# A four-layer gated network on one core: context work of three sequences kept for the sorted experts of layer 0, their rare branch issued first, and a denser schedule of table writes in layer 1

## The chip, the core and the metric

The kernel runs on one core of a Trainium2 chip, in one launch. The time is what the device takes for one execution, in microseconds (us). Before the change it is 2764.47 us in the median of three runs (2760.23 to 2768.61).

The engines in the profile are PE (matrix products, with its weight loads listed as PEld), DVE (vector), ACT (activations), POOL (GpSimd) and SP, which only issues DMAs. Each works through its own list of instructions in order. Lists are laid down when the kernel is built: the scheduler gives every instruction a priority by its place in the program, takes the first one that is ready by its own reckoning, and writes the semaphore waits that correctness needs.

## What is computed

Eight sequences of 256 tokens, 512 channels wide, pass through four layers. Each layer adds a gated attention over a context of the same shape, then a gated feed-forward part. Only layer 0 and the first half of layer 1 bear on the change:

```python
x = x + tanh(g_xattn[0]) * L0_xattn(layernorm(x), ctx)      # 16 heads, 8-bit rounding of the queries and the output
x = x + tanh(g_ffn[0])   * L0_ffn(layernorm(x))             # 8 experts of rank 64, each token takes the best one
x = x + tanh(g_xattn[1]) * L1_xattn(layernorm(x), ctx)      # linear attention
x = x + tanh(g_ffn[1])   * L1_ffn(layernorm(x))             # 64 experts, each token takes 8
...
# L1_xattn
k_prime = relu(key_heads @ Wkf.T)                            # 64 features a head
kv      = einsum('bhnf,bhne->bhfe', k_prime, v)
out     = einsum('bhmf,bhfe->bhme', q_prime, kv) / (q_prime . k_sum + 1e-8)
```

The keys, features and sums (`k_prime`, `kv`) of layer 1's linear attention depend on the context alone, not on the tokens.

## The kernel before

The tokens are held in 16 tiles `xt` of 128 tokens. Three stages follow one another: `front` (layer 0), `middle` (layer 1) and `back` (layers 2 and 3). Much of the kernel is written as Python generators: work that is off the main path is cut into pieces by `yield`, and the main path calls `next` on it at chosen points. A piece that is called early comes early in the program, and so has priority over what is called later.

**Attention of layer 0.** `attend0` (L773 on) takes one sequence: four groups of four heads, each with score products (L796), a masked maximum on DVE (L816), exponentials on ACT (L821), turns on PE (L828) and products with the values (L837). After each head it calls `step`, 16 times in a sequence. `step` moves the projection of the sequence before (`proj`) by one piece and, at the sequence's `rate`, the generator `others(b)` by one piece or two. `others` mixes what the next sequence needs (queries, keys, values), the routing `route0` of the one before, and the context work `linear(b - 1)` for b of 2 to 7.

**Context work.** `linear(b)` (L374 on) makes layer 1's keys (two pieces, products L219, ACT L329), values (two pieces, DVE L384), features (two pieces, products L398, DVE L406) and sums (two pieces, products L421, DVE L428) of sequence b, and stores the sums in DRAM as `kvd[b]` (L430), from where layer 1 loads them (L1094). Eight pieces and a store in all. The last sequence's is the generator `last_side`: one piece goes into the projection of the last sequence, two into its routing, the rest into `sorted0`.

**Sorted experts.** `route0` writes, for two tiles of tokens at a time, number and weight of each token into rows of a table in DRAM, by indirect DMAs on POOL (L513). `sorted0` counts the tokens of each expert (L624), reads the slices of the table that are used (L647), turns them on PE (`who_ps`, L678) into `who` and `share`, and goes over tiles of 128 tokens in pairs. Each tile is gathered by an indirect DMA on POOL (L688) and turned (L197); `up` (L715) and `down` (L727) are the two products; the result is scaled (L734, L736) and written to `res0` in DRAM by an indirect DMA on POOL (L737). Eight pairs are fixed, two more always run with expert weights gathered on POOL (L702), and up to ten further tiles stand in a branch, `tc.If(tiles > MORE0_ANY)`, at the end. Its condition is a count that each engine loads into a register of its own. Where the branch is not taken, each engine adds to the semaphores what the skipped part would have added; POOL first waits for its own open DMAs.

**From layer 0 to layer 1.** `results0`, called from `attend1` of the first block, reads `res0` back (L1077, SP) and adds it to the tokens: the first four tiles on DVE, the other twelve on POOL (both L1085). Small tiles of layer 1 lie in memory that tiles of layer 0 had, so they wait until those are free.

**Layer 1.** `attend1` takes four blocks of 512 tokens. It calls `step(n)` after each part, 20 writes' worth in a block; a call moves `work()`, the routing `route1` of earlier half blocks (13 pieces for each of seven), by one piece, and issues up to n writes to layer 1's table (L1188, indirect DMAs on POOL, 128 in all, 16 for each half block). `hurry`, in the second half of the last block, makes that two rounds. Each write waits for the newest product (`latest`). Each routing begins with a norm that needs a power on POOL (L172). After the blocks, the rest of `work()` runs, then the shared expert of three blocks in 13 pieces with up to three writes behind each; the routing of the last half block goes beside it and then writes all that is left. The table is read on POOL (L1422), turned on PE (L1438), and layer 1's experts begin.

Of the kernel before, what the change touches and what calls it, by code (L numbers as in the profile page):

```python
# [11 lines left out]
F32 = mybir.dt.float32  # L12
# [3 lines left out]
ALU = mybir.AluOpType  # L16
# [4 lines left out]
P = 128  # L21
# [26 lines left out]
def flamingo_kernel(ctx: ExitStack, tc: tile.TileContext, a):  # L48
# [214 lines left out]

    def front():
# [51 lines left out]

        def keys(b, bank, w=None, bias=None, out=None, name="k0"):

            out = K if out is None else out
            w, bias = (wkT, bk) if w is None else (w, bias)  # L320
            out[b] = qkv.tile([P, KC, S], F32, tag="qkv", name=f"{name}_{b}")
            for h in range(2):
                ps = bank(f"{name}ps{b}_{h}").rearrange("p (n t) -> p n t", n=2)
                for n in range(2):
                    j = 2 * h + n
                    matmul_k(ps[:, n], [w[:, k, ts(j, P)] for k in range(KC)], [ctxs[b][:, k, :] for k in range(KC)])
                for n in range(2):
# [50 lines left out]
        def linear(b, bank):  # L378

            yield from keys(b, bank, wk1, bk1, K1, "k1")  # L380
            for lt in range(2):
                ps = bank(f"v1_{b}_{lt}")
                matmul_k(ps, [ctxs[b][:, k, ts(lt, P)] for k in range(KC)], [wv1[:, k, :] for k in range(KC)])
# [156 lines left out]
        def others(b):  # L540
# [17 lines left out]
            def context():  # L558
                if b + 1 < B:
                    yield from keys(b + 1, actile)  # L560
                    yield from values(b + 1, actile)
                if b > 1:
                    yield from linear(b - 1, actile)
# [24 lines left out]
        rate = (0.9, 0.9, *(5 * (1.7,)), 1.3)  # L588
        last_side = linear(B - 1, mmtile)
# [18 lines left out]
        for n, _ in enumerate(proj[0]):  # L608
            if n == 1:
                next(last_side)  # L610
# [3 lines left out]
        for n, _ in enumerate(rest):  # L614
            if n in (1, 2):
                next(last_side)
        sorted0(AB, xnd, table, halves, writes, run, onesb, side, part, pair_no, more_no, is_more, tile_no, last_side)

    def sorted0(AB, xnd, table, halves, writes, run, onesb, lp, part, static_row, more_no, is_more, tile_no, filler):
# [54 lines left out]
        next(filler)  # L674
        next(filler)
# [46 lines left out]

        def down(nm, hT, Bs, ns, free=True):
            ps = [mmtile(f"y0_{nm}_{n}") for n in range(2)]
            last = None
            for n in range(2):
                one = nc.tensor.matmul(ps[n], hT[half[n], :], Bs[n], start=True, stop=True)  # L727
                if last is not None:
                    behind(one, last, "two experts side by side")
                last = one  # L730
            for n, i in enumerate(ns):
# [17 lines left out]

        rest = None  # L750
        static = [(c, t) for t in range(2) for c in range(4)]
        for c, t in static:
# [6 lines left out]
            next(filler, None)  # L759

        def more_pair(m, rest, free):
            ns = [16 + m, 16 + m + 1]
            xgTs = [gathered(i) for i in ns]
            ws = [weights(m + n) for n in range(2)]
            hT = up(f"m{m}", xgTs, [w[0] for w in ws])
            if rest is not None:
                down(*rest)
            return f"m{m}", hT, [w[1] for w in ws], ns, free
# [3 lines left out]
        down(*rest)  # L772
        for _ in filler:  # L773
            pass
        with tc.If(tiles > MORE0_ANY):
            rest = None
            for m in range(MORE0_ANY, MORE0, 2):
                rest = more_pair(m, rest, False)
            down(*rest)
# [168 lines left out]
    def middle():  # L948
        with ExitStack() as st:
# [123 lines left out]
            def results0(tiles, eng):  # L1073

                for t in tiles:
                    more = t2.tile([P, C], F32, tag="t2", name=f"res0_{t}")
                    load = nc.sync.dma_start(more, res0[ts(t, P), :])  # L1077
                    for one in done0:
                        tc.add_manual_dep(
                            load.ins,  # L1080
                            one.ins.name,
                            mybir.DependencyInfo(mybir.DependencyClass.Sync, mybir.DependencyReason.DATA),
                            reason="every token's result is there",
                        )
                    eng.tensor_tensor(out=xt[t], in0=xt[t], in1=more, op=ALU.add)  # L1085
# [1293 lines left out]
```

## Time and profile before

| | |
|---|---|
| median of three runs | 2764.47 us |
| the profiled execution | 2741.27 us |
| its span, first to last instruction | 2739.6 us |
| mean granted PE clock | 0.961 |
| PE busy | 2504.7 us, 91% |
| PE weight loads busy | 1371.3 us, 50% |
| DVE busy | 1302.5 us, 48% |
| POOL busy | 979.8 us, 36% |
| ACT busy | 678.1 us, 25% |

The profiled execution is 23 us faster than the median of the runs beside it; parts of it are to be compared with each other, not with the median.

Stages in this execution: layer 0's attention to 567 us, its routing and experts to 661, layer 1's attention from 685 to 905, layer 1's shared expert and last routing to 971, its experts from 1010 on. DMA engines are busy for 0.9 and more of the time in the experts of layer 1 and for under 0.25 in both attentions. Layer 1's 128 table writes take 126.9 us on POOL, 991 ns each in the mean, with 0.3 us between two that follow one another; the 16 result loads of layer 0 land 4.6 us after issue in the median.

A timeline line gives start, duration, engine, line of the program, instruction, output and inputs, shape and count, and in brackets the idle time before it with what ended it. PE's ends are modelled, and neighbouring products overlap in it.

### The profile page before, as it was taken

The page shows a single profiled execution, that of the slowest core. Times are in us where ns is not written, and L with a number is a line of the kernel's source. Part 1 is how long each engine was busy: PE and PEld are TensorE (multiplying, and loading weights), DVE is VectorE, ACT ScalarE, POOL GpSimd, SP SyncE. Part 2 cuts the span into 40 slices and gives each one's busy share as a digit, 9 for nine tenths or more (in the row PEclk, how much of TensorE's full clock was granted, in tenths as well). Part 3 has the DMA queues.
Part 4 walks back from the last instruction along what each step waited for, and adds up shares of the span by engine and source line. Part 5 has one row for each costly group of instructions (what it writes and reads, how often), then busy time and mean ns, then how long its engine had stood idle before and what let it go on. Part 6 is the DMA issues. An engine that isn't in the chain of part 4 may idle for free. (4 is left out here: it accounts for less than half of the span.)

```text
span 2739.6 us, 29988 instructions
## 1 busy us (share of the span) xinstructions
PE 2504.7 (91%) x10207; PEld 1371.3 (50%) x10215; DVE 1302.5 (48%) x3652; ACT 678.1 (25%) x1567; POOL 979.8 (36%) x915
## 2 busy tenths in 40 slices
PE   8888888966999839999999899899999899999997
PEld 6555555543555415555555344444444444455554
DVE  6666666543476812222222471567677765111111
ACT  2443434311112203232323220222212221111110
POOL 1121111136344665555555210131434252433332
PEclk9999999978799869999999999999999999999999
DMA  5000001045121228999998542112022211788984
GB/s 214 13 12 24 24 24 47 16 115 180 36 78 51 78 97 219 232 243 237 245 230 227 139 189 73 58 70 100 31 92 79 99 34 46 240 283 270 300 278 112
DMA packets 107942, 351.79 MB, mean 128 GB/s; under 512 B 23759, under 2 KB 26321, under 8 KB 100869
## 3 DMA queue, kind: packets, MB, share of 16 engines
q0 software_dynamic: 49920, 166.53, 23.8%
q1 hardware_dynamic: 54596, 178.99, 18.5%
q10 hardware_dynamic: 3264, 4.24, 0.5%
q8 instruction: 86, 1.41, 0.2%
q14 instruction: 76, 0.61, 0.1%
HBM read 289.47 MB, written 76.66 MB: 134 GB/s over the span
## 5 line engine op out<-in xcount | busy, mean ns | idle before, releaser
L219 PE MATMUL gu<-w,eb 128*128 128x352 f32 x896 | 286.4, 463 | 0.0
L1541 POOL DMA_INDIRECT acc<-eb,who x112 | 176.9, 1580 | 189.9 <-ACT eb L110 165.7
L219 PE MATMUL h2p<-xnT_f,p 128*128 128x512 f32 x512 | 226.2, 596 | 6.7 <-issue 6.0
L219 PE MATMUL o2f<-p,h 128*128 128x512 f32 x512 | 226.0, 595 | 3.5 <-ACT h L1699 3.4
L219 PEld LDWEIGHTS gu<-w,eb 128*128 128x128 f32 x896 | 162.5, 192 | 73.6 <-issue 2.3
L821 ACT ACTIVATE pr<-pr,n 128x256 f32<-128x256 f32 x256 | 128.4, 503 | 152.4 <-DVE n L816 133.4
L219 PEld LDWEIGHTS h2p<-xnT_f,p 128*128 128x128 f32 x512 | 96.7, 191 | 123.9 <-issue 121.3
L219 PEld LDWEIGHTS o2f<-p,h 128*128 128x128 f32 x512 | 95.7, 190 | 122.8 <-issue 114.7
L1188 POOL DMA_INDIRECT table<-pay,rowi x128 | 126.9, 991 | 83.7 <-issue 29.7
L1461 POOL DMA_INDIRECT xg<-xnd,who x112 | 116.5, 1040 | 49.6 <-PE ehp L1488 19.2
L197 PEld LDWEIGHTS tr_xg<-ident,xg 128*128 128x128 f32 x672 | 77.0, 142 | 111.9 <-issue 55.2
L197 PE MATMUL tr_xg<-ident,xg 128*128 128x128 f32 x672 | 116.5, 285 | 8.2 <-DMA xg<-xnd,who 8.2
L1532 PE MATMUL ed<-w,eb 128*128 128x512 f32 x224 | 116.1, 600 | 0.9 <-DVE eb L1489 0.9
L2043 PE MATMUL g_r<-w,xgT 128*128 128x352 f32 x288 | 111.2, 468 | 0.8 <-DVE xgT L108 0.8
L230 DVE SCALAR_TENSOR_TENSOR x<-o2f,tg,x 128x512 f32<-128x512 f32 x64 | 46.9, 741 | 136.8 <-PE o2f L219 135.3
L2043 PE MATMUL u_r<-w,xgT 128*128 128x352 f32 x288 | 108.7, 459 | 0.0
L816 DVE CUSTOM_DVE_ANT_0 pr<-s,mask 128x256 f32<-128x256 f32 x256 | 99.1, 417 | 13.5 <-PE s L796 5.9
L2066 PE MATMUL d_r<-w,hT_r 128*128 128x512 f32 (+1 forms) x216 | 104.2, 592 | 0.0
L1478 DVE SCALAR_TENSOR_TENSOR eb<-eb,share,gu 128x176 f32<-128x176 f32 x112 | 44.0, 393 | 121.1 <-ACT eb L1477 121.1
L108 DVE COPY eb<-ed 128x512 f32<-128x512 f32 x56 | 38.7, 692 | 129.9 <-PE ed L1532 129.9
L1699 ACT ACTIVATE h<-h2p,b 128x512 f32<-128x512 f32 x64 | 43.4, 687 | 215.9 <-PE h2p L219 215.7
L828 PE MATMUL pt<-ident,pr 128*128 128x128 f32 x512 | 88.9, 290 | 6.9 <-ACT pr L821 3.6
(702 smaller groups left out, 4722.3 us busy)
## 6 DMA issues: line engine op xcount, KB each, us to landing
w<-in_w SPq DMA_DIRECT2D x64, 960.0 KB, 6.9
p<-in_p SPq DMA_DIRECT2D x64, 512.0 KB, 5.4
xnd<-xn_f SPq DMA_DIRECT2D x32, 256.0 KB, 3.0
acc<-xnd SPq DMA_DIRECT2D x32, 256.0 KB, 4.6
more<-acc SPq DMA_DIRECT2D x32, 256.0 KB, 5.3
wd<-in_wd SPq DMA_DIRECT2D x64, 96.0 KB
ctx<-in_ctxT SPq DMA_DIRECT2D x8, 512.0 KB, 3.5
x<-in_x SPq DMA_DIRECT2D x16, 256.0 KB, 6.0
```

The source lines that it names most:

```text
L197: one = nc.tensor.transpose(ps[:, k, :], src[:, ts(k, P)], ident)
L219: one = nc.tensor.matmul(ps, lhsT[k], rhs[k], start=(k == 0), stop=(k == n - 1))
L230: return nc.vector.scalar_tensor_tensor(xt[i], ps, scale, xt[i], ALU.mult, ALU.add)
L816: one = nc.vector.tensor_tensor_reduce(pr[:, nt, :], ps[r][:, nt, :], mask[:, nt, :], -1.0, -LOW, ALU.add, ALU.min, n16[:, nt, h : h + 1],)
L821: nc.scalar.activation(pr[:, nt, :], pr[:, nt, :], AF.Exp, bias=n16[:, nt, h : h + 1], scale=-1.0, accum_out=s16[:, nt, h : h + 1],)
L828: nc.tensor.transpose(pt_ps[:, lt, nt, :], pr[:, nt, ts(lt, P)], ident)
L1188: one = nc.gpsimd.indirect_dma_start(out=table[:, :], out_offset=bass.IndirectOffsetOnAxis(ap=rows, axis=0), in_=choice, in_offset=None, b ...
L1461: nc.gpsimd.indirect_dma_start(out=xg, out_offset=None, in_=xnd[:, :], in_offset=bass.IndirectOffsetOnAxis(ap=who[:, c : c + 1], axis=0), ...
L1532: one = nc.tensor.matmul(ps[n], t.hT[rows, k, :], wd, start=(k == 0), stop=(k == 1))
L1541: nc.gpsimd.indirect_dma_start(out=acc[n][:, :], out_offset=bass.IndirectOffsetOnAxis(ap=who[:, t.c : t.c + 1], axis=0), in_=t.x, in_offse ...
L2043: nc.tensor.matmul(ps[:, 0:I3], xTt[:, k, :], wgu[k][:, g, :], start=(k == 0), stop=(k == KC - 1))
L2066: one = nc.tensor.matmul(ps, hT[:cn, n, :], wd[n][:cn], start=(n == 0), stop=(n == 2))
```

## The change

It has five parts.

1. `others` no longer runs `linear` for b of 6 and 7, so the context work of sequences 5 and 6 is not in layer 0's attention. `last_side` runs over sequences 5, 6 and 7. The rates of the last two sequences go from 1.7 and 1.3 to 1.3 and 0.5.
2. Its pieces are spread anew: five in the last projection (one before), three in the last routing (two before), which together are sequence 5; seven behind the table's read (two before); none between the fixed pairs of experts (one for each before); the other nine behind the last pair. The key and value products of these last ones are ordered on PE behind the last `down` product (`hold`, `held`).
3. The branch is issued ahead of the fixed pairs, not behind everything.
4. The first four tiles' `results0` is called in `sorted0`, behind the last pair and ahead of those nine pieces. The other twelve stay where they were.
5. In layer 1's attention a call of `step` moves the routing by 1.4 pieces (2 with `hurry`, as before) and issues up to 2n writes.

```diff
@@ front
+        hold = []
+        def held(one):
+            for other in hold:
+                behind(one, other, "the experts first")
...
-                    matmul_k(ps[:, n], [w[:, k, ts(j, P)] for k in range(KC)], [ctxs[b][:, k, :] for k in range(KC)])
+                    one = matmul_k(ps[:, n], [w[:, k, ts(j, P)] for k in range(KC)], [ctxs[b][:, k, :] for k in range(KC)])
+                    held(one)
...
-                if b > 1:
+                if 1 < b < B - 2:
                     yield from linear(b - 1, actile)
...
-        rate = (0.9, 0.9, *(5 * (1.7,)), 1.3)
-        last_side = linear(B - 1, mmtile)
+        rate = (0.9, 0.9, *(4 * (1.7,)), 1.3, 0.5)
+        last_side = (x for b in range(B - 3, B) for x in linear(b, mmtile))
...
         for n, _ in enumerate(proj[0]):
-            if n == 1:
+            if n:
                 next(last_side)
...
         for n, _ in enumerate(rest):
-            if n in (1, 2):
+            if n in (0, 1, 2):
                 next(last_side)
@@ sorted0
-        next(filler)
-        next(filler)
+        for _ in range(7):
+            next(filler)
...
+        with tc.If(tiles > MORE0_ANY):
+            rest = None
+            for m in range(MORE0_ANY, MORE0, 2):
+                rest = more_pair(m, rest, False)
+            down(*rest)
+
         rest = None
         static = [(c, t) for t in range(2) for c in range(4)]
         for c, t in static:
...
-            next(filler, None)
...
         for m in range(0, MORE0_ANY, 2):
             rest = more_pair(m, rest, True)
         down(*rest)
+        results0(range(TB), nc.vector)
+        hold.append(latest_down[0])
         for _ in filler:
             pass
-        with tc.If(tiles > MORE0_ANY):
...
@@ middle
-                if blk == 0:
-                    results0(range(TB), nc.vector)
...
             gen = work()
+            due = [0.0]
             def step(n, hurry=False):
-                for _ in range(2 if hurry else 1):
-                    next(gen, None)
-                    write(n, latest[0])
+                due[0] += 2.0 if hurry else 1.4
+                while due[0] >= 1.0:
+                    due[0] -= 1.0
+                    next(gen, None)
+                write(2 * n, latest[0])
```

`results0` itself is the same text, moved to where both stages can call it. `more_pair` is moved up without a change. Two lines say what waits for what: `matmul_k` returns the first of its products, so `held` orders that one, and those that follow accumulate behind it; `results0` makes each load wait for every scatter in `done0`, which are those of the fixed pairs and the two that always run.

More of the change, by code (lines that the diff above doesn't have):

```diff
@@ L261, in spread, with results0 @@
         nc.tensor.matmul(ps, ones, d, start=True, stop=True)
+    def results0(tiles, eng):
+        for t in tiles:
+            more = t2.tile([P, C], F32, tag="t2", name=f"res0_{t}")
+            load = nc.sync.dma_start(more, res0[ts(t, P), :])
+            for one in done0:
+                tc.add_manual_dep(
+                    load.ins,
+                    one.ins.name,
+                    mybir.DependencyInfo(mybir.DependencyClass.Sync, mybir.DependencyReason.DATA),
+                    reason="every token's result is there",
+                )
+            eng.tensor_tensor(out=xt[t], in0=xt[t], in1=more, op=ALU.add)
     def front():
@@ L382, in linear @@
                 ps = bank(f"v1_{b}_{lt}")
-                matmul_k(ps, [ctxs[b][:, k, ts(lt, P)] for k in range(KC)], [wv1[:, k, :] for k in range(KC)])
+                one = matmul_k(ps, [ctxs[b][:, k, ts(lt, P)] for k in range(KC)], [wv1[:, k, :] for k in range(KC)])
+                held(one)
                 nc.vector.tensor_tensor(
@@ L614, in front, with sorted0 @@
         for n, _ in enumerate(rest):
-            if n in (1, 2):
+            if n in (0, 1, 2):
                 next(last_side)
-        sorted0(AB, xnd, table, halves, writes, run, onesb, side, part, pair_no, more_no, is_more, tile_no, last_side)
-    def sorted0(AB, xnd, table, halves, writes, run, onesb, lp, part, static_row, more_no, is_more, tile_no, filler):
+        sorted0(
+            AB, xnd, table, halves, writes, run, onesb, side, part, pair_no, more_no, is_more, tile_no, last_side, hold
+        )
+    def sorted0(AB, xnd, table, halves, writes, run, onesb, lp, part, static_row, more_no, is_more, tile_no, filler, hold):
         A, Bw = AB
@@ L721, in up @@
             return hT
+        latest_down = []
         def down(nm, hT, Bs, ns, free=True):
@@ L730, in down @@
                 last = one
+            latest_down[:] = [last]
             for n, i in enumerate(ns):
@@ L748, in down, with more_pair @@
                     done0.append(one)
+        def more_pair(m, rest, free):
+            ns = [16 + m, 16 + m + 1]
+            xgTs = [gathered(i) for i in ns]
+            ws = [weights(m + n) for n in range(2)]
+            hT = up(f"m{m}", xgTs, [w[0] for w in ws])
+            if rest is not None:
+                down(*rest)
+            return f"m{m}", hT, [w[1] for w in ws], ns, free
+        with tc.If(tiles > MORE0_ANY):
+            rest = None
+            for m in range(MORE0_ANY, MORE0, 2):
+                rest = more_pair(m, rest, False)
+            down(*rest)
         rest = None
@@ L758, in sorted0 @@
             rest = (f"{c}_{t}", hT, [Bw[half[n], c, :] for n in range(2)], ns)
-            next(filler, None)
[L761 to L768, printed above, removed]
         for m in range(0, MORE0_ANY, 2):
@@ L772, in sorted0 @@
         down(*rest)
+        results0(range(TB), nc.vector)
+        hold.append(latest_down[0])
         for _ in filler:
             pass
-        with tc.If(tiles > MORE0_ANY):
[L776 to L779, printed above, removed]
     def attend0(b, Q, K, V, woT, gswo, gbo, aos, owed, last_max, step):
@@ L1071, in middle @@
             heads4 = [slice(HD * r, HD * r + HD) for r in range(4)]
[L1073 to L1085, printed above, removed]
             def attend1(blk, one_step):
                 step = one_step
-                if blk == 0:
-                    results0(range(TB), nc.vector)
                 kvs = []
```

## The prediction

> **What bounds it now.** I read the page's slices first, for stages in which no engine is full. Each column is one fortieth of the span, 68.5 us.
>
> ```profile
> PE   8888888966999839999999899899999899999997
> DVE  6666666543476812222222471567677765111111
> POOL 1121111136344665555555210131434252433332
> ```
>
> TensorE (PE) sits at 8 or 9 nearly everywhere: it is the bound. It falls to 6 in slices 9 and 10 (layer 0's experts) and to 3 in slice 14 (before layer 1's experts), so time can be had there. Then I cut the span at the starts of score products and at the edges of PE's pauses. Columns: stretch, its length, busy time and count of PE, weight loads, DVE, ACT and POOL, granted clock, DMA share, GB/s.
>
> ```profile
> 91.00:149.00 58.00, 48.08 (x345) 29.52 (x350) 40.82 (x139) 27.00 (x86) 12.20 (x12) 0.97 0.05 18
> ...
> 366.00:438.00 72.00, 65.29 (x437) 43.50 (x442) 46.12 (x158) 28.11 (x91) 12.63 (x12) 0.98 0.06 20
> 438.00:508.00 70.00, 61.52 (x421) 40.75 (x416) 43.05 (x149) 27.17 (x86) 11.93 (x11) 1.00 0.12 42
> 508.00:567.00 59.00, 55.16 (x382) 36.21 (x384) 36.65 (x134) 25.71 (x86) 9.87 (x9) 0.91 0.06 20
> 567.00:592.00 25.00, 19.37 (x93) 10.58 (x92) 13.90 (x43) 3.44 (x8) 5.74 (x5) 0.93 0.53 173
> 592.00:608.40 16.40, 0.44 (x2) 0.31 (x2) 2.70 (x20) 0.18 (x1) 9.84 (x10) 0.55 0.58 125
> 608.40:660.60 52.20, 48.69 (x328) 30.05 (x328) 17.04 (x29) 13.48 (x25) 34.41 (x34) 0.95 0.44 151
> 660.60:685.10 24.50, 0.00 (x0) 0.00 (x0) 10.03 (x39) 0.28 (x1) 11.31 (x18) 0.59 0.63 229
> 685.10:905.00 219.90, 203.00 (x1036) 123.50 (x1037) 141.10 (x646) 43.37 (x77) 92.95 (x88) 0.92 0.22 62
> 905.00:971.50 66.50, 62.15 (x176) 27.61 (x174) 48.58 (x272) 11.11 (x14) 47.90 (x50) 0.90 0.18 57
> 971.50:1010.20 38.70, 0.13 (x1) 0.00 (x0) 0.85 (x2) 0.59 (x1) 26.86 (x28) 0.56 0.03 4
> ```
>
> Three stretches have almost no PE work: 16.4, 24.5 and 38.7 us. PE's timeline says what ends each (start, duration, instruction, idle before it and its releaser):
>
> ```profile
> 603.62 0.44 PE L678 MATMUL who_ps<-ident,slots 30*128 30x30 f32 x2 [11.70 <-DMA slots<-table,row_t]
> 608.42 1.11 PE L197 MATMUL tr_xg<-ident,xg 128*128 128x128 f32 x4 [4.37 <-DMA xg<-xnd,who]
> ...
> 685.17 3.00 PE L197 MATMUL tr_a<-ident,xn_a 128*128 128x128 f32 x12 [24.64 <-DVE xn_a L182]
> ...
> 1010.25 0.70 PE L1438 MATMUL who_ps<-ident,rows 128*128 128x128 f32 x2 [38.62 <-DMA rows<-table,row_c]
> ```
>
> The first waits for layer 0's table, then for the gathered rows; the second for the experts' results, their sum and the norm; the third for layer 1's table. POOL's timeline shows why the third is long:
>
> ```profile
> 663.31 0.98 POOL L737 DMA_INDIRECT res<-y_m,who  x1 [0.30 <-issue]
> 667.73 0.20 POOL L993 MEMSET before<- 128x128 bf16 x1 [3.43 <-DMA res<-y,who]
> ...
> 1004.32 0.97 POOL L1188 DMA_INDIRECT table<-pay,rowi  x1 [0.30 <-issue]
> 1007.48 0.99 POOL L1422 DMA_INDIRECT rows<-table,row_c  x1 [2.19 <-issue]
> ```
>
> From 920.72 to 1004.32 POOL issues 66 table writes back to back, 83.6/65 = 1.29 us apart. The table can be read only behind the last; PE resumes 1010.25 - 1004.32 = 5.9 us after that one's start.
>
> **Part 1, context work out of attention.** One sequence's context work (`linear`) on PE, from undisturbed runs in the timeline: K 32 products at 3.62/16 = 7.2 us, V 16 at 4.45/10 = 7.1, features 2 x 1.16 = 2.3, sums 2 x 2.0 = 4.0; 20.6 in all. Sequences start at 90.89, 148.72, 437.70 and 507.92. The second, without `linear`, takes 57.8; the sixth, with it, 71.7; the seventh 70.2. So the seventh should gain 70.2 - 57.8 = **12.4**. The eighth loses its `linear` too and has little other filler; I take the mean price seen, 72 - 57.8 = **14.2**, between 6 (if its own chain of scores, exponentials and turns is what sets it) and 20.6 (all of the PE work). The lower step rates only spread what is left. Sum **-26.6** (-18 to -33).
>
> **Part 2, the projection and routing tail (567 to 592).** Before it holds K, V and half the features of the last sequence (15.4 us); after it holds the whole of sequence 5 (20.6): 5.2 more, into 25.0 - 19.4 = 5.6 of idle time that is cut small by the chain. **+3** (0 to 5.3).
>
> **Part 3, the wait for the table.** Seven steps of sequence 6 are issued ahead of the turning of the table: 7.2 + 7.1 + 2.3 + 2.0 = 18.6 us. Before, from the count (591.73) to the first turned tokens (608.42) took 16.7. The filler is ready earlier and stands first in PE's order, so the turn comes after it; then the gather's 608.42 - 603.62 = 4.8 is bare, since the held filler is not allowed there. 18.6 + 4.8 - 16.7 = **+6.7** (down to +1.9 if the turn slips in between and the gather is covered). Behind the late turn wait POOL's gathers, and nobody else.
>
> **Part 4, the branch.** It moves from behind the experts to ahead of them, between the token list and the gathers. Not taken, it makes POOL wait for its own open DMAs. Bounds: ACT goes from its last result (end 660.89) to its next DMA behind the branch (661.00), 0.1 us; POOL waits 3.4, which is its last scatter landing. At its new place the table read has already landed and the four early weight gathers, issued by 603.4, nearly so: **+1** (0.1 to 3.4). [...]
>
> **Part 5, layer 0's experts.** 40 gathers and scatters at 1.02 + 0.30 = 1.32 take 52.8 of POOL's 59.7 us (604.62 to 664.29): POOL sets this stage. The 5.7 us of filler that ran inside leave; they can give back at most POOL's 6.9 of idle. If the four weight gathers (1.28 each) no longer pass ahead into the table's wait, they add 5.2. **-2** (-6.9 to +5.2).
>
> **Part 6, the results.** The first four result loads move ahead of the filler in program order and wait only for the scatters; sequence 7 (20.6 us) and the last step of sequence 6 (2.0) run behind the last down product. The chain from there to the first turn stays 24.6 (scatter landed by 667.4, loads, sums, statistics, norm); the filler's 22.6 fits inside. **0**; -2 if the chain gets shorter, because the loads no longer queue on SP behind the constants of the next layer (670.28 instead of 667.4). If the norm's small tiles lie where sequence 7's K still lives, the norm starts only when the filler ends: 22.6 + 8.7 (676.44 to 685.17) - 24.6 = +6.7.
>
> Front in all: -26.6 + 3 + 6.7 + 1 - 2 = **-17.9**.
>
> **Part 7, more table writes.** Walking through the step calls: before, the four attention blocks pop 53 of the 128 writes and 15 steps of routing are left over; after (1.4 routing steps per call, twice the writes) they pop 92, and none is left. So 39 writes, 39 x 1.29 = 50 us of POOL, leave the jam. Of the 36 that remain, 20 take 26 us from 905 and are done by about 938; the last 16 come with the last tokens' choices, which DVE finishes in two halves (952.8 and 961.0). The first eight run 952.9 to 963.1, the last one starts at 972.0, PE resumes 5.9 later: 978.0 instead of 1010.25, **-32.2**. If routing that was done earlier frees DVE so that the last tokens end sooner, the whole pause goes: -38.6. If the last tokens slip by a dozen us, -20.
>
> **What pays for it (685 to 905).** POOL goes from 93 to 143 busy us of 220 there, DVE takes over the 15 steps. POOL works in order, and each norm needs a power on POOL (3 for attention, 7 for routing); now DVE waits 3.3 + 3.0 us in all for these. One more write ahead of each of ten is 10 x 1.29 = 12.9; nothing if they find gaps. **+3** (0 to 12.9), nearer the present waits. A table write takes 0.97 us in the median and 1.35 at most here, among DVE work. [...]
>
> **Sum.** -17.9 - 32.2 + 3 = **-47.1** against the profiled execution, 2741.3 us (span 2739.6), gives 2694.2. The median of the runs shown, 2764.5, lies 23.2 above that execution; nothing in the change bears on the difference, so I carry it: **2717**.
>
> **Rivals.** (a) *Only the writes count.* The filler moved to the front's pauses pushes the chains there as much as attention gains: parts 1 to 6 come to 0. For it: the tail, turn and norm are chains, and 41 us of work is put into some 46 of idle time. Against: PE was at 90% in the seventh sequence, so removed work must show. -29.2: **2735**. (b) *Only the front counts.* The last tokens' choices come so late, or the writes find so little room in the blocks, that the third pause stays: -17.9, **2747**. Against: POOL has 127 idle us of 220 there. (c) *Slower: POOL's queue takes over in layer 1's attention.* Four writes per call, each waiting for a product, stand ahead of a power; DVE waits for it in order, and PE for DVE. At five writes (6.4 us) for each of ten norms it costs 64 instead of 3: -47 + 61 = +14, **2778**. It decides from (50.1 + 8.3)/10 = 5.8 us a norm. For it: a write waited 16.7 us for a product once. Against: the longest wait for a power now is 1.1 us. (d) *The change does not do it:* the scheduler, which may hoist what is ready, already spreads work so that the order stays: 2764.
>
> **Chances.** 0.66 for the forecast (its own range 2697 to 2733), 0.04 for still better, (a) 0.10, (b) 0.07, (c) 0.09, (d) 0.04. A measurement of this kernel can tell about 0.3%, 8.3 us, from no change. Faster 0.66 + 0.04 + 0.10 + 0.07 = 0.87, same 0.04, slower 0.09. All best ends together would give 2686, all worst 2767; I take 2692 to 2748, which leaves out (c), (d) and a few of the best.
>
> **What would show it.** Part 1: seventh and eighth sequences of 58 and 45 us. Part 3: no pause at the table's turn, one of about 5 at the first turned tokens. Part 6: the 24.6 pause replaced by K, V, feature and sum products. Part 7: some 90 writes on POOL before the last attention block ends, a pause before layer 1's table under 10 us. Wrong: idle time on DVE released by the powers on POOL above 20 us in layer 1's attention, or the turn of the table standing in front of its filler.

## Result, and the profile after

The changed kernel took 2791.26 us in the median of 6 runs (2780.48 to 2796.03), the kernel before 2760.74 (2752.46 to 2768.61, 6 runs): ratio 1.0104, 95% interval 1.0078 to 1.013, some 30 us slower. The profiled executions were 2792.27 us (span 2790.6) and 2741.27 us (span 2739.6). Jobs came in two kinds, whatever the kernel: in one the kernel before takes 2739 to 2744 us in the median, in the other 2758 to 2761. So every ratio below is against the kernel before in the same job (the ratios are not quotients of the two medians, and differ a little from them). The profile of before is of the first kind; the profile after and the runs of this comparison are of the second (the last section shows the marks).

The slices of the changed kernel, each 69.8 us:

```profile
PE   8888988877788788999999999999999999999998
PEclk9999999887877889999999999999999999999999
```

The 3 of PE in slice 14 is gone: the pause before layer 1's table has been taken away. But slices 10 to 13 (counted from 0), layer 1's attention, fell from 9 and 8 to 7 and 8, and the granted clock (PEclk) is 7 and 8 there too. Next come stretches of the profile after: the seventh sequence of layer 0's attention; the eighth with its tail, up to the count of layer 0's table; layer 0's experts; from there to the first Q product of layer 1; layer 1's attention, from that product to the end of the last output product; and what is behind it, up to the last pause. Columns: stretch, length, busy time and count of PE, weight loads, DVE, ACT, POOL, granted clock, DMA share, GB/s.

```profile
444.30:497.30 53.00, 42.80 (x295) 25.74 (x292) 35.59 (x135) 23.88 (x78) 11.66 (x11) 0.94 0.17 57
497.30:583.00 85.70, 72.22 (x447) 47.63 (x445) 49.10 (x177) 30.28 (x96) 15.77 (x14) 0.82 0.15 41
...
602.00:667.00 65.00, 52.60 (x281) 30.39 (x281) 14.71 (x24) 13.27 (x24) 37.38 (x37) 0.78 0.48 156
667.00:710.60 43.60, 26.11 (x145) 19.49 (x145) 22.24 (x53) 3.54 (x7) 27.34 (x31) 0.79 0.49 166
710.60:994.30 283.70, 236.37 (x1063) 145.40 (x1064) 156.26 (x777) 45.41 (x78) 113.83 (x114) 0.83 0.18 47
994.30:1052.20 57.90, 53.09 (x133) 21.65 (x132) 26.64 (x134) 5.81 (x8) 36.02 (x37) 0.88 0.24 66
```

The kernel before, the eighth sequence with its tail, then layer 1's attention and what is behind it, up to the turn of layer 1's table:

```profile
507.90:591.70 83.80, 74.44 (x472) 46.80 (x474) 50.53 (x176) 29.25 (x94) 15.61 (x14) 0.92 0.20 65
...
691.00:912.50 221.50, 206.39 (x1037) 123.67 (x1038) 142.06 (x670) 42.20 (x75) 92.73 (x90) 0.93 0.21 60
912.50:1010.20 97.70, 54.79 (x161) 24.41 (x159) 43.98 (x244) 11.70 (x15) 69.09 (x71) 0.77 0.14 41
```

The first Q product of layer 1 came at 710.6 instead of 691.0 (+19.6). Layer 1's attention, from there to the end of the last output product, took 283.7 us instead of 221.5 (+62.2): PE is busy 30 us longer for nearly the same products (1063 for 1037; granted clock 0.83 for 0.93), and idle 32 us longer. From there to the turn of layer 1's table it took 62.2 instead of 97.8 (-35.6). The rest is +4.8. PE's timeline at the places that the prediction named, and at the new pauses:

```profile
595.31 0.42 PE L703 MATMUL who_ps<-ident,slots 30*128 30x30 f32 x2 [0.22 <-DMA slots<-table,row_t]
601.92 1.09 PE L197 MATMUL tr_xg<-ident,xg 128*128 128x128 f32 x4 [3.96 <-DMA xg<-xnd,who]
702.28 3.04 PE L197 MATMUL tr_a<-ident,xn_a 128*128 128x128 f32 x12 [12.91 <-DVE xn_a L182]
812.17 1.94 PE L197 MATMUL tr_f<-ident,xn_f 128*128 128x128 f32 x8 [5.15 <-DVE xn_f L182]
838.59 0.27 PE L1282 MATMUL pos<-sel,before 128*128 128x128 bf16 x1 [5.74 <-DVE sel L1268]
1056.51 0.70 PE L1455 MATMUL who_ps<-ident,rows 128*128 128x128 f32 x2 [4.35 <-DMA rows<-table,row_c]
```

The pause at layer 0's table is gone (0.22 for 11.70), the one at layer 1's table fell from 38.62 to 4.35. The one ahead of the first norm of layer 1 is 12.91 although 22 us of filler now stand in front of it. And there are pauses of 5 us at `tr_f` (turns of tokens normed for routing) and at `pos` (positions of the choices). PE's waits there in layer 1's attention (us in total, times, longest), before and then after; before has none at `pos`:

```profile
PE tr_f L197 <- DVE xn_f L182: 1.2, 1, 1.2
```

```profile
PE tr_f L197 <- DVE xn_f L182: 17.2, 4, 5.6
PE pos L1282 <- DVE sel L1268: 12.6, 3, 5.7
```

### The profile page after: what moved, and what is told of

It reads as the page before. It is cut to its first block, busy times and chain, and to the rows that moved or that the text cites. A ratio compares the mean times of both kernels' runs of the same rounds, so it can differ in the third digit from the quotient of the medians.

```text
span 2790.6 us, 29997 instructions
## 1 busy us (share of the span) xinstructions
PE 2558.1 (92%) x10215; PEld 1404.6 (50%) x10215; DVE 1302.4 (47%) x3652; ACT 677.3 (24%) x1565; POOL 978.5 (35%) x915
## 5 line engine op out<-in xcount | busy, mean ns | idle before, releaser
L2277 POOL DMA_INDIRECT out_dram<-y_r,who x36 | 58.0, 1612 | 109.6 <-issue 53.0
```

Of the source, the lines that this page charges most:

```text
L2277: nc.gpsimd.indirect_dma_start(out=a["out"][:, :], out_offset=bass.IndirectOffsetOnAxis(ap=who[:, n : n + 1], axis=0), in_=y, in_offset=No ...
```

## The experiments

Attention is layer 1's, from the first Q product to the end of the last output product; behind it is from there to the turn of layer 1's table. Both from the profiled execution, in us. The first two rows are the profiles of the kernels before and after.

| run | kernel | median us | ratio to before in its job (95%) | first Q | attention | behind it |
|---|---|---|---|---|---|---|
| | before | | | 691.0 | 221.5 | 97.8 |
| | after | 2791.3 | 1.0104 (1.0078 to 1.013) | 710.6 | 283.7 | 62.2 |
| e1 | step alone | 2748.5 | 1.0024 (1.0009 to 1.004) | 686.0 | 270.8 | 57.3 |
| e2 | front alone | 2740.2 | 0.9993 (0.998 to 1.0007) | 687.3 | 216.1 | 98.6 |
| e3 | writes alone | 2729.5 | 0.9958 (0.9942 to 0.9973) | 696.1 | 220.6 | 82.1 |
| e4 | rate alone | 2758.3 | 1.0061 (1.0042 to 1.0081) | 691.8 | 267.1 | 72.5 |
| e5 | after again | 2794.0 | 1.0131 (1.0111 to 1.015) | 711.1 | 289.8 | 62.0 |
| e6 | after, rate back | 2778.6 | 1.0092 (1.0069 to 1.0115) | 707.6 | 238.0 | 94.4 |
| e7 | e6, sums later | 2773.1 | 1.0057 (1.0036 to 1.0077) | 700.3 | 244.8 | 97.0 |
| e8 | after, gaps | 2786.9 | 1.011 (1.0087 to 1.0133) | 710.6 | 281.1 | 62.1 |
| e9 | before again | 2759.7 | 1.0001 (0.9983 to 1.0019) | 688.9 | 218.1 | 113.0 |
| e10 | front alone | 2770.0 | 1.0022 (1.0005 to 1.0039) | 704.6 | 227.2 | 110.1 |
| e11 | writes alone | 2767.8 | 1.0017 (1.0 to 1.0035) | 695.4 | 245.9 | 95.8 |
| e12 | step, lag | 2763.1 | 1.001 (0.9988 to 1.0033) | 701.7 | 243.9 | 88.4 |
| e13 | step, writes unbound | 2764.6 | 1.0093 (1.0062 to 1.0124) | 691.3 | 267.0 | 72.6 |
| e14 | before, writes unbound | 2747.9 | 1.0036 (1.0014 to 1.0057) | 693.9 | 221.4 | 102.2 |
| e15 | step alone | 2744.5 | 1.0017 (1.0001 to 1.0034) | 688.2 | 268.6 | 57.3 |
| e16 | rate alone | 2756.1 | 1.0047 (1.0028 to 1.0067) | 696.3 | 260.8 | 72.6 |
| e17 | after again | 2745.5 | 1.0022 (1.0007 to 1.0037) | 689.4 | 265.8 | 57.2 |
| e18 | e7 again | 2729.0 | 0.9946 (0.9925 to 0.9966) | 689.3 | 225.9 | 82.1 |

Jobs: e1 to e4 (before 2743.8 us), e5 to e8 (2758.3), e9 to e12 (2760.8), e13 to e16 (2739.5), e17 and e18 (2739.3).

### Step, front, writes, rate (e1 to e4)

Theory 1 was that the new rate of routing pieces costs, theory 2 that the added table writes on POOL do. The edits, on the kernel before: e1 takes the new `step` as a whole, e3 only `write(2 * n, ...)` in the old loop, e4 the new loop with `write(n, ...)`. e2 is the changed kernel with the old `step`.

```diff
+            due = [0.0]
             def step(n, hurry=False):
-                for _ in range(2 if hurry else 1):
+                due[0] += 2.0 if hurry else 1.4
+                while due[0] >= 1.0:
+                    due[0] -= 1.0
                     next(gen, None)
-                    write(n, latest[0])
+                write(2 * n, latest[0])
```

> The kernel before with only the new step: 1.4 routing pieces a call and twice the writes. If the middle's loss comes from the step itself (both theories of it), layer 1's attention from the first Q product to the end of the last wo product takes 270 to 285 us instead of 221, the pause before layer 1's table falls from 38.6 to under 8, and the time is 2770 to 2790. If the loss needs the late start that the new front gives (transfers and constants of layer 1 squeezed together), attention stays below 235 and the time is 2725 to 2740.

> The changed kernel with the old step: only the parts ahead of layer 1 are changed. By the two traces the first Q product comes 19.6 us later than before, layer 1's attention takes 221 again and the pause before the table is 38.6 again: 2775 to 2785. The recorded prediction's front sum of -17.9 would give 2743; if the 20 us by which the profile of before lies under its median sit in the front, 2755 to 2765.

> The kernel before with twice the writes per step, but one routing piece a call as before. By the walk through the step calls the attention blocks pop 70 writes instead of about 50, so the pause before the table shrinks by some 20 x 1.29 = 26 us. Theory 1 (the rate of routing pieces makes PE's turns and position products stand right behind the DVE and POOL work they need): attention stays within 221 to 230, the time is 2735 to 2745. Theory 2 (POOL's queue: the writes stand ahead of the norms' powers): attention takes over 250, PE's waits for the normed tokens stay above 12 us, and the time is 2770 to 2800.

> The kernel before with 1.4 routing pieces a call, but the old number of writes per call. The walk pops about 56 writes, so the pause before the table stays above 28 us. Theory 1 (rate): attention takes 265 to 285, with PE waiting some 5 us each for normed tokens and for the choices, and the time is 2795 to 2815. Theory 2 (POOL's queue): attention stays within 221 to 235, and the time is 2750 to 2770.

Attention and the stretch behind it, for e3 and then e4:

```profile
696.10:916.70 220.60, 202.32 (x1037) 119.25 (x1038) 142.15 (x670) 42.20 (x75) 106.30 (x104) 0.95 0.22 61
916.70:998.80 82.10, 55.35 (x162) 24.49 (x160) 43.98 (x244) 11.70 (x15) 55.09 (x57) 0.83 0.16 48
```

```profile
691.80:958.90 267.10, 232.78 (x1063) 143.48 (x1064) 156.82 (x762) 44.22 (x78) 109.61 (x108) 0.83 0.18 50
958.90:1031.40 72.50, 49.90 (x133) 20.68 (x132) 30.44 (x151) 6.99 (x10) 50.42 (x52) 0.84 0.20 54
```

The expected times were reckoned from a before of 2761 us, and before took 2744 in this job, so differences are to be compared. Twice the writes (e3) cost attention nothing here and save 16 us behind it: -14.3 us, where theory 1 expected -16 to -26. The rate alone (e4) makes attention 46 us longer, as theory 1 expected, but saves 25 behind it, since routing done early is not done late: +14.5, not +34 to +54. Both together (e1): attention 270.8, pause 4.65, +4.7, the attention and the pause as expected, the sum below the +9 to +29 reckoned. The front alone (e2) gives -3.6, neither the +14 to +24 read off the two traces nor the -18 of the prediction. So theory 1 holds for the sum. Theory 2 is not quite out, as one pause shows. First the changed kernel: DVE has the statistics ready (`ve_f`), POOL takes the power (`rstd_f`), DVE norms (`xn_f`), and PE, idle since 807.0, turns at 812.17.

```profile
805.15 0.74 DVE L230 SCALAR_TENSOR_TENSOR x<-wo,tg,x 128x512 f32<-128x512 f32 x1
...
807.46 0.15 DVE L170 TENSOR_SCALAR ve_f<-mv_f 128x2 f32<-128x2 f32 x1
...
811.48 1.00 DVE L182 TENSOR_SCALAR xn_f<-x,mv_f,rstd_f 128x512 f32<-128x512 f32 x2 [3.28 <-POOL rstd_f L172]
...
808.43 0.97 POOL L1202 DMA_INDIRECT table<-pay,rowi  x1 [0.30 <-issue]
809.71 0.97 POOL L1202 DMA_INDIRECT table<-pay,rowi  x1 [0.30 <-issue]
810.70 0.75 POOL L172 TENSOR_TENSOR rstd_f<-ve_f,mhalf 128x2 f32<-128x2 f32 x1
```

And the same place of e4, with half the writes:

```profile
786.77 0.72 POOL L172 TENSOR_TENSOR rstd_f<-ve_f,mhalf 128x2 f32<-128x2 f32 x1 [3.75 <-DVE ve_f L170]
...
788.22 1.09 PE L197 MATMUL tr_f<-ident,xn_f 128*128 128x128 f32 x8 [2.08 <-DVE xn_f L182]
```

Two things meet. The norm is of sums that were made just before (`x<-wo` at 805.15, statistics right behind): the routing has caught up with attention, and its whole chain lies bare: 2.08 us in e4. And in the changed kernel the power stands behind two writes (ready at 807.6, run at 810.7): 3.1 us more, 5.15 in all.

With the old number of writes the queue on POOL can do more than that. The last turns in e4's attention:

```profile
923.31 0.17 DVE L170 TENSOR_SCALAR ve_f<-mv_f 128x2 f32<-128x2 f32 x1
...
940.70 0.74 POOL L172 TENSOR_TENSOR rstd_f<-ve_f,mhalf 128x2 f32<-128x2 f32 x1
...
942.08 1.97 PE L197 MATMUL tr_f<-ident,xn_f 128*128 128x128 f32 x8 [14.98 <-DVE xn_f L182]
```

Thirteen table writes, issued back to back from 924.39 to 939.72, stand between the statistics and the power: some 13 of these 15 us are POOL's queue, as theory 2 says, and e16 has the same pause (14.97). Twice the writes per call leave fewer for the end, and the pause is 5.6 in e1. So "rate alone" is not free of theory 2. But the rate is needed for either: with one piece a call no pause at `tr_f` is over 1.3 us, with the old writes (e2, e9, e10) or with twice as many (e3, e6, e7, e11, e18), and with 1.4 every run but e12 (below) has three of 2 to 15.

### What the pauses cost besides (the clock)

In e4 PE idles 34.3 us in attention, 15.1 in before: 19 of the 46 us. The granted clock (last but two) has the rest; first the changed kernel ahead of, in and behind the pause at 812.17, then e4 in the pause at 788.22 and behind it:

```profile
801.00:807.00 6.00, 6.00 (x39) 2.64 (x37) 5.79 (x31) 0.76 (x2) 2.92 (x3) 1.00 0.01 0
807.00:812.20 5.20, 0.05 (x2) 0.06 (x1) 1.92 (x5) 1.03 (x2) 3.67 (x4) 0.98 0.03 2
812.20:829.30 17.10, 17.03 (x69) 14.04 (x70) 7.62 (x44) 2.05 (x4) 6.35 (x7) 0.51 0.45 102
829.30:832.80 3.50, 3.50 (x10) 1.39 (x9) 0.77 (x2) 0.00 (x0) 2.58 (x4) 1.00 0.13 38
```

```profile
786.10:788.20 2.10, 0.04 (x1) 0.01 (x1) 1.85 (x5) 0.46 (x1) 0.72 (x1) 1.00 0.00 0
789.40:806.50 17.10, 17.03 (x63) 13.35 (x63) 6.79 (x41) 1.53 (x4) 6.31 (x7) 0.50 0.32 99
```

Behind a pause of 5 us, and behind one of 2, PE works almost without a break for 17.1 us at a granted clock of 0.51 and 0.50. By estimate, half of 17.1, that is some 8 us of work lost behind each, the long pause and the short one. PE's busy time in attention says the same: 206.4 us in before, 232.8 in e4, for 26 products more in 1063. But the price does not go with the pause alone. In e4 the pause of 1.99 us ahead of `pos` at 811.94 is followed by 3.4 us at half clock. In before, one of 1.19 us ahead of the first `tr_f` at 725.95 is followed by 13.7. And in e12 (below) PE is at half clock for 13.7 us where no pause near it is above 0.8:

```profile
813.30:816.70 3.40, 3.40 (x13) 2.29 (x12) 3.40 (x11) 0.59 (x1) 1.16 (x1) 0.50 0.02 3
```

```profile
726.60:740.30 13.70, 13.51 (x56) 11.41 (x55) 6.77 (x34) 2.73 (x4) 2.28 (x2) 0.50 0.41 135
```

```profile
789.00:802.70 13.70, 10.96 (x38) 8.03 (x38) 6.71 (x36) 2.06 (x4) 11.10 (x12) 0.50 0.12 21
```

The four long stretches hold the small products `qkv` (66 columns) between turns; the short one holds output products (512 columns) and turns. Whether the pause or these products set the length was not tried.

### The whole change beside its parts (e5 to e8)

e5 is the changed kernel. e6 gives it the old loop with `write(2 * n, ...)`. e7 adds to e6 an order for the sums of results on POOL, behind the first norm's power. e8 keeps 1.4 and lets a call end where a norm, or the choices, have just been issued (`break` on a mark that `route1` yields there).

```diff
-            eng.tensor_tensor(out=xt[t], in0=xt[t], in1=more, op=ALU.add)
+            one = eng.tensor_tensor(out=xt[t], in0=xt[t], in1=more, op=ALU.add)
+            for other in after:
+                behind(one, other, "the norm first")
...
-                results0(range(TB, TT), nc.gpsimd)
+                results0(range(TB, TT), nc.gpsimd, power)
```

```diff
                 while due[0] >= 1.0:
                     due[0] -= 1.0
-                    next(gen, None)
+                    if next(gen, None) == "gap":
+                        break
```

> The changed kernel once more, beside its parts on one chip. If the parts simply add (step alone +4.7 us, front alone -3.6 us against before), it lies 1 us above before, between -5 and +7. If the front and the step hinder each other, as the first comparison of +30 suggests, it lies 20 to 35 us above before and layer 1's attention takes 280 to 285 us instead of the 271 of the step alone.

> The changed kernel with one routing piece a call again (two where it hurries), and twice the writes kept. Theory 1 (the routing rate of 1.4 is what costs): layer 1's attention takes 216 to 222 us, the pauses of PE for normed tokens and choices are gone, the pause before layer 1's table is about 22, and the time is 14 to 22 us below before. Theory 2 (POOL's queue, full of writes): attention stays above 250 and the time lies above before.

> The kernel of e6 with one edit of order: the twelve sums of results on POOL stand behind the first norm's power. If these sums (9 in a row, 11 us, ahead of the constants that DVE waits for) are what keeps layer 1's first norm late, the 13 us pause ahead of the first turned tokens shrinks to between 1 and 9 us and the time is 4 to 12 us below that of e6. If the norm waits for the filler's memory instead, the pause stays within 2 us of 13 and so does the time.

> The changed kernel with the rate of 1.4 and twice the writes, but a call never goes on from a norm to its turns, or from the choices to their positions: it stops there, and the rest of its due is done in later calls. Theory 1 in its narrow form (PE's turns and positions stand right behind the DVE and POOL work they need): the 5 us pauses go, layer 1's attention takes 230 to 245 us instead of 271 to 284, the pause before the table stays under 10, and the time is 20 to 45 us below the changed kernel's. If the cost is the number of routing pieces in attention as such, attention stays above 262 and the time within 8 us of the changed kernel's.

This job was of the other kind, and the parts of the first job do not add in it: the whole change is 1.31% above before. With the old rate, attention loses 52 of its 290 us (e6), but is 238, not 222, and the time is above before, not below: a miss. e8 missed too: the pauses stood as before.

```profile
812.47 1.94 PE L197 MATMUL tr_f<-ident,xn_f 128*128 128x128 f32 x8 [5.15 <-DVE xn_f L182]
```

So the narrow form of theory 1, that turns are issued in the very call that issues the norm, is out. What is left is that the norm itself starts too late. e7 lies within its range: the pause ahead of the first norm's turns fell from 13.28 to 7.30, the time by 5.5 us. What it mends is seen in the changed kernel:

```profile
681.93 11.06 POOL L276 TENSOR_TENSOR x<-x,res 128x512 f32<-128x512 f32 x9 [8.78 <-DMA res<-res]
...
693.76 0.14 POOL L1041 IOTA cs<- 128x1 f32 x1
...
693.93 0.15 DVE L1042 TENSOR_SCALAR cs<-cs 128x1 f32<-128x1 f32 x1 [7.29 <-POOL cs L1041]
...
694.25 0.68 DVE L163 BATCH_NORM_STATS2 bn_a<-x 128x6 f32<-128x512 f32 x1
```

The four sums that the first norm needs were done by 681. But its statistics stand on DVE behind a constant (`cs`), which waits for POOL's half of it, which stands behind nine sums that nobody needs yet.

### Before, front and writes in that kind of job, and the lag (e9 to e12)

e9 is the kernel before, e10 the one of e2, e11 the one of e3. e12 is e1 with routing one sequence later:

```diff
-                    while q not in done:
+                    while len(done) < q + 2:
                         yield
```

> The kernel before, for a second profile on the chip of its partners: within 0.3% of before, layer 1's attention 218 to 224 us, 38 us of pause ahead of layer 1's table. If the profile of before that the prediction used was a quick execution in its front, the first Q product comes later than 691 us, at 695 to 712.

> The front alone once more, beside before and the writes alone. If the front costs what the first comparison of the whole change says (+30 less the 5 of the step), it lies 10 to 30 us above before, with more half-clock windows in the last two sequences of attention and in the experts; if it is what the first batch showed, it lies within 6 us of before.

> Twice the writes alone once more: 10 to 18 us below before on any chip, if the shorter pause ahead of the table is what it gains and layer 1's attention stays within 4 us of before's; above before by 5 us or more if twice the writes need a gap that only the first chip's execution left.

> The kernel before with the new step (rate 1.4, twice the writes), but the routing of a sequence begins only when the sequence after it has also been projected. If the cost of the rate is that routing catches up with attention, so that PE's turns wait for a norm of sums that have just been made, the 5 us pauses ahead of turned tokens go, layer 1's attention takes 221 to 235 us instead of 271, the pause ahead of the table is 5 to 16 and the time is 10 to 25 us below before. If the pauses come from the number of routing pieces per call or from POOL's queue alone, attention stays above 255 and the time lies above before.

In this kind of job twice the writes are no gain: attention grows by 28 us over e9 in the same job, and behind it 17 are won. The front alone comes out above before (+0.22%, 9 us by the medians), between its two ranges. e12, for attention and behind it:

```profile
701.70:945.60 243.90, 218.06 (x1038) 131.85 (x1039) 143.63 (x685) 42.85 (x75) 104.42 (x103) 0.87 0.19 55
945.60:1034.00 88.40, 60.63 (x161) 25.99 (x159) 40.51 (x220) 9.14 (x13) 52.52 (x54) 0.79 0.16 45
```

```profile
782.29 1.09 PE L197 MATMUL tr_f<-ident,xn_f 128*128 128x128 f32 x8
```

With the lag the rate costs attention nothing: 243.9 us, beside 245.9 for the writes alone in this job, and the turns no longer wait (the row has no idle time ahead of it). The expected 221 to 235 and the gain were missed by what the writes cost here. The unlagged step alone was not run in this job; under the new front it took 289.8 in this kind of job (e5), and 270.8 and 268.6 alone in the other (e1, e15). The lag does two things at once: it keeps each norm away from the sum that it reads, and it sends most of the added routing back behind attention (DVE has 685 instructions there, 762 in e4, 670 in before). That the first is what counts is argued from where the pauses stand, at the turns and positions themselves; the amount by itself was not tried.

### Writes out of attention, step and rate once more (e13 to e16)

e13 and e14 set `write(0 * n, ...)` in the step of e1 and of before, so that all writes are issued behind attention in the program. e15 and e16 are the kernels of e1 and e4.

> The kernel before with the rate of 1.4, but no table write inside attention: all 128 come behind it. If PE's 5 us pauses are 2 us of norm and choices and 3 us of powers queued behind writes on POOL, the pauses ahead of turned tokens and positions are 1.5 to 2.3 us each, and attention takes 250 to 268 us on account of the half-clock stretches behind them. If the rate by itself costs nothing and the writes all, attention stays within 216 to 228. The stage behind attention grows by 92 writes x 1.28 = 118 us at most, and the time lies 50 to 120 us above before.

> The kernel before with no table write inside attention. DVE has no idle time there that nothing explains, attention takes 212 to 221 us, and the stage behind it grows by 53 writes x 1.28 = 68 us at most: 35 to 70 us above before. If attention gets shorter than before's by more than 6 us, before's own writes already cost that.

> The step alone once more, beside e13, e14 and e16. On a chip where DVE stands still during bursts of writes: attention 275 to 290 us, the time 10 to 30 us above before. On one where it does not: attention 268 to 273 us, 2 to 8 us above before, as in the first batch.

> The rate of 1.4 with the old number of writes, on the chip of e13 to e15. Between e13 and e15: attention 262 to 282 us, PE's pauses at turned tokens and positions 2 to 4 us, the time 10 to 35 us above before.

e13 and e14 did not do what they were made for: writes that no product holds back were moved up by the scheduler, and 78 and 58 of them still ran inside attention, as many as in e4 (78) and nearly as many as in before (60). e13 shows only that unbound writes in front of a power can be worse: waits of 7.37, 9.81 and 13.67 us at three `tr_f`. What writes cost attention by themselves was not isolated. e15 and e16 repeat e1 and e4: 268.6 and 260.8 us, +5.1 and +16.6 us. e16 missed in its pauses: the longest is 14.97 us, not 2 to 4, and attention is 1 us under the range.

### The whole change in the first kind of job, and the best version (e17, e18)

> The whole change. In a job in which DVE does not stand still (before about 2742 us): the parts add, 5 us below to 8 us above before, layer 1's attention 262 to 274 us. In one in which it does (before about 2760): 28 to 38 us above before, attention 282 to 292, as in the second job.

> The front, twice the writes, one routing piece a call, and the sums on POOL behind the first norm's power. In a job of the first kind front -4, writes -14 and the sums -5 add to 18 to 28 us below before, with attention 214 to 222; it is then the fastest of all. In one of the second kind it lies 10 to 20 us above before, as e7, and some 20 below the whole change.

```profile
689.40:955.20 265.80, 229.59 (x1063) 141.71 (x1064) 156.27 (x777) 44.41 (x78) 113.68 (x114) 0.85 0.18 51
955.20:1012.40 57.20, 50.44 (x133) 20.94 (x132) 28.44 (x137) 6.99 (x10) 36.97 (x38) 0.92 0.22 69
```

Here the parts nearly add: step +5, front -4, the whole +6.2 us, within the range expected. e18 is the fastest against before in its job (0.9946), and beats the changed kernel in both kinds of job (e7 against e5). It gained 10 us, not the expected 18 to 28; its attention took 225.9, a few us longer than expected, and it lies within the interval of the writes alone (e3), so that no gain of the front shows in it. In the other kind of job no version tried beats the kernel before.

## Why the prediction was wrong

The step that failed is **"What pays for it (685 to 905)": +3 (0 to 12.9)**. It measured +44 (e17 against the profile of before, one kind of job) to +62 (the profile on record). The prediction took the fifteen routing steps that come into attention as work for DVE that finds room, and priced only ten more writes ahead of ten powers. It did not ask what 1.4 pieces a call mean: ten calls per sequence give 14 pieces, a sequence's routing has 13, so that routing no longer lags, and each norm for routing follows the sum it reads. The runs put in its place: the rate with the old writes, +39 to +46 us of attention (e16, e4), with one jam of writes ahead of a power in it; twice the writes on top, +4 to +8 (e1 less e4, e15 less e16), as they lengthen most pauses and shorten that one; with one piece a call (e3, e18) or with the lag (e12) no such pause. What the prediction did price, DVE's wait for the powers, went from 6.3 to 22.4 us (e17), also past its upper bound of 12.9 more. And the clock was missing from the price: PE was busy 26 us longer in e4's attention for 26 products more.

**Part 7, -32.2:** right. The pause fell by 34.3, and the profile after counts 92 writes in attention, as walked through (in before it counts 60, where the walk gave 53). With the routing that left, the stretch behind attention lost 40.6 us in e17 (97.8 to 57.2).

**Parts 1 and 2, -26.6 and +3:** the sum is off by only 5 us, but by luck. The count product came at 591.5 us (mean of eight profiles with the old front, all of the first kind of job) and at 572.6 with the new (e2, e17, e18): -18.9 instead of -23.6. By the same means the seventh sequence lost 18.4 us (71.2 to 52.8), more than the 12.4 forecast, and the eighth with its tail up to the count gained 1.1 (82.9 to 84.0), where -14.2 and +3 were forecast. The rows above show the latter: PE has 25 products fewer there (447 for 472), but at a granted clock of 0.82 instead of 0.92 it is busy nearly as long, and it idles 4 us more. Also, 18 of the 32 key products of sequence 6, which the prediction put behind the count, ran ahead of it. In the profile after the count is only 8.7 us earlier, since its seventh sequence began 6.6 us later than in before (444.3 for 437.7), behind sequences that the change does not touch.

**Part 3, +6.7:** wrong order. The turn did stand in front of the last piece of its filler, the case given as "if the turn slips in between", and those 18 key products were out of its way. The first turned tokens came 17.4 us earlier than with the old front by the same means: +1.5 instead of +6.7.

**Parts 4 and 5, +1 and -2:** the experts took 54.2 us in e2 for 52.1, inside the bounds. In the profile after they took 65.0, outside them: pauses of 4.6 and 4.7 us, and a granted clock of 0.78. Some of this is the kind of job, in which the old front took 58.0 there (e9).

**Part 6, 0 (-2 to +6.7):** the step of the front that failed. From the last down product to the first turn: 24.6 before, 35.8 in e2, 35.3 in the profile after: +11. Not the memory of the norm's tiles, but the order on DVE and POOL, as e7 shows for some of it (6.0 of the pause's 13.3 us; in e18 2.5 of e17's 12.65). What is left in e18, 10.12 us, follows the filler's own sums and a loaded row on DVE, and was not tried.

Front in all: -17.9 predicted, -3.5 at the first Q product in e2 and e17 against the eight, and -3.6 us in the runs of e2.

**The carry of 23.2 us** was wrong: "nothing in the change bears on the difference". The profile of before and its timed runs were of two kinds of job, and in that of the runs the front and the writes cost time (e10, e11).

**Rivals.** (c) came nearest, with its sign right and its place right. In the changed kernel POOL's queue is 3 us of a 5 us pause, and twice the writes make no such pause without the rate; in e4 and e16 it is most of the longest one. Its mark, idle time of DVE at the powers above 20 us, was just met in e17 (12.8 us at `xn_f`, 9.6 at `xn_a`). (a) was right in that the front comes to next to nothing. (b) and (d) fall: the writes moved, the pauses too.

**Writes and clock.** A table write on POOL took as long as before: 0.98 us in the mean of 128 in the profile after, 0.99 in before. What stood still, in one kind of job, was DVE (below). The prediction has no term for a lower clock behind a pause. In e4 2.1 us of idle time were followed by 17.1 us at a granted clock of 0.50, in before 1.2 us by 13.7, and PE's rows show hardly a break in them. What sets the clock, and how long it stays low, was not shown.

## What to carry to other kernels

Before raising the rate of filler work in a loop, count what it supplies against what becomes ready: filler that catches up with its producer turned here into a chain of waits on the bound engine (17.2 us at `tr_f` and 12.6 at `pos` in the profile after, 1.2 and none in before). Price a pause of TensorE with the clock that follows it, and look at which products run there: by estimate from e4's windows, 2.1 us of waiting with half of 17.1 us at a clock of 0.50 cost some 10 ahead of turns and 66-column products, and 2.0 us with half of 3.4 under 4 ahead of 512-column ones. And a filler put in front of a critical chain did not hide it here, as the chain's own first steps stood behind it, or behind work that nobody needed yet, on another engine's queue: from the last down product to the first turn it took 35.3 us with the filler and 24.6 without.

## What was not expected of the hardware

Two kinds of jobs showed, and two chips had both at different times (number 8 in the second and fourth job, 11 in the third and fifth). In the second kind DVE stands still where nothing that the profile shows holds it (17.54 us at one place of e9). The kernel before, the same instruction in the profile used for the prediction and in e9:

```profile
931.81 0.29 DVE L1283 TENSOR_TENSOR key<-pos,e 128x128 f32<-128x128 f32 x1 [0.22 <-PE pos L1271]
```

```profile
931.39 0.17 DVE L1277 RECIPROCAL wden<-wden 128x2 f32<-128x2 f32 x1
949.10 0.29 DVE L1283 TENSOR_TENSOR key<-pos,e 128x128 f32<-128x128 f32 x1 [17.54 <-issue]
```

```profile
688.90:907.00 218.10, 197.95 (x1037) 117.53 (x1038) 142.59 (x669) 42.20 (x75) 91.25 (x89) 0.96 0.21 61
907.00:1020.00 113.00, 63.65 (x163) 27.41 (x160) 44.68 (x244) 11.70 (x15) 70.23 (x72) 0.74 0.13 35
```

In these 17.5 us POOL issues table writes back to back (sixteen starts from 930.26 to 949.44), and the second of the two products that DVE needs had started at 929.78. Where writes run on, DVE then does one or two short steps per write (969.23, 970.66, 972.05). Over the 113 us DVE has 35 us of idle time that the profile puts down to no engine of the core; in the profiles of the first, fourth and fifth job it has 0.2 behind attention. So e9 spends in waits what the profile of before spends in one pause of 38.6 ahead of the table (5.3 in e9), and 15 us more. That the writes are the cause is the author's guess from their place alone; it was not shown, since the runs made for it moved too few writes and fell into the other kind of job. What makes a job of the one or the other kind stays open.
